# Conv + Fourier mixer + quantized FFN on one core: tokens parked in DRAM, two x buffers, and the forward sum over h in 64x64 tiles

## The chip, the cores and the metric

The kernel runs on one core of one Trainium2 chip. The metric is the device time of one launch in microseconds. All 32 images of the batch go through this one core.

## What is computed

The reference has two layers. Layer 0 is an inverted bottleneck with weights mixed per image; layer 1 is a Fourier mixer over the tokens and a feed-forward network (FFN) with numbers rounded to fp8 (e5m2). Cut to what matters:

```python
# x: (32, 56, 56, 96)
rw  = sigmoid(mean(x, (1, 2)) @ Wr + br)             # 4 routing weights per image
Wk  = einsum('be,ecm->bcm', rw, Wpw)                 # mixed pointwise weights
h   = relu(bn1(einsum('bhwc,bcm->bhwm', x, Wk)))     # 96 -> 384
h   = relu(bn2(depthwise3x3(h, mixed taps)))
x   = bn3(einsum('bhwm,bmf->bhwf', h, Wk2)) + x      # 384 -> 96, residual

t   = tokens(x)                                      # (32, 3136, 96)
a   = relu(bn(layernorm(t) @ w1.T))                  # 96 -> 192
X   = fft(a, axis=tokens, norm='ortho')
y   = ifft(relu(re) + 1j * relu(im), norm='ortho').real   # re, im: diagonal r, i, and biases
t   = t + bn(y @ w2.T)
t   = t + q_ffn(layernorm(t))                        # 96 -> 384 -> 96, fp8 operands
```

The Fourier transform over the 3136 = 56 x 56 tokens is done in two steps: a sum over h for each of the 56 columns w (29 frequencies, since the input is real), then a sum over w.

## The kernel before

**Layout.** x of an image lies as 96 channels x 3136 tokens in SBUF. There are three such buffers (`xpad`, `xs`, image b in buffer b % 3). Layer 0 overwrites x with its own output, the Fourier part adds to it, the FFN adds to it, and from there it is stored to the output. So a buffer belongs to one image from its load to the last store.

**Stages of one image**, each a Python generator that issues instructions:

- `loads` loads x; `mixing` sums x over the tokens on DVE (`pooled`), makes the routing weights (`ps_rw`), and the mixed weights `wk`, `small`, `wk2`.
- `expansion` (`ps_pw`), evicted by `expanded` into `hp`; the depthwise convolution partly on TensorE in 32x32 tiles (`convolved_tensor`, `ps_dw`) and partly on DVE (`convolved_vector`, `h2`); `projection` (`ps_pwl`), evicted by `projected`.
- `forward`, for four strips of 784 tokens: `moments` transposes the tokens (`ps_t_a`), takes `bn_stats` and makes one over the standard deviation (`rstd_a`). Then `ps_w1`: 112 tokens (two columns w) x 192. DVE scales and clips it into `ha`. Then `ps_a`: the sum over h with the matrix `dfta_s`. ACT copies it to `g`, and SP stores it to DRAM (`gd`).
- `frequency_loads` reads `gd` back in another order into `g2`; `frequencies` does the sum over w (`ps_b`), then `nonlinearity`, then `spectrum` (`ps_w2`, `ps_c`), stored to DRAM (`yd`).
- `inverse`: reads `yd` (`yt`), sums back (`ps_d`), adds it to x, normalizes (`ps_t_f`, `nt8`, `ps_n`), runs the FFN (`ps_f1`, `hidden`, `ps_f2`), adds it and stores the output.

**Order.** The order of the instructions on every engine is fixed when the program is built. `Plan.run` holds all generators, estimates when each could go on, and takes the one that can start first (priorities break ties). Inside one period, the convolution of image b stands among the forward part of b-1 and b, the frequency part of b-1 and the inverse of b-2. Every engine then works through its own queue in that order, held by semaphores.

**Padding.** PSUM has four tiles of two banks. `psum` takes one, and where `Plan` expects TensorE to be idle it first issues products that nobody reads:

```python
for _ in range(min(40, int((plan.idle() - 0.3) / 0.19))):
    nc.tensor.matmul(ps[:PB, 0:PB], dftb_s, dftb_s, start=True, stop=True)
```

**Lines.** Most instructions are issued by helpers, so the profile gives them one line: L553 is `mm`, L557 `transpose`, L321 the padding in `psum`, L282 every recorded instruction of DVE, ACT, POOL and SP. After the change the same helpers stand at L584, L588, L328 and L289.

**Before the loop**, the constants are loaded on the SP queue, among them the Fourier matrices `dfta_s` and `dftd_s` (1421 KB each). Scratch for this lies in the pool `prep`; the pools `mix` and `strip` are opened after `prep` is closed.

Of the kernel before, what the change touches and what calls it, by code (L numbers as in the profile page):

```python
# [56 lines left out]
PA = 4 * K1  # L57
KR = 2 * K1
# [3 lines left out]
SQ = SW // 2  # L62
T = SW * S
# [13 lines left out]
GK = 8  # L77
GROUPS = [(0, 16), (16, 13)]
# [52 lines left out]
class Plan:  # L131
# [8 lines left out]
    TAIL = {PE: 0.2, DVE: 0.12, ACT: 0.14, POOL: 0.1, SP: 0.0}  # L140

# [57 lines left out]
    def run(self):  # L199
        while self.streams:  # L200
            best = None
            for stream in self.streams:
                if any(len(self.buffers[tag]) < n for tag, n in stream.takes.items()):
                    continue
                ready = stream.ready
                missing = False
                for key in stream.after:
                    at = self.events.get(key)
                    if at is None:
                        missing = True  # L210
                        break
                    ready = max(ready, at)
                if missing:
                    continue
                for tag, n in stream.takes.items():
                    ready = max(ready, self.buffers[tag][n - 1])
                key = (max(ready, self.free[stream.engine]), stream.priority, ready)
                if best is None or key < best[0]:
                    best = key, ready, stream
            if best is None:  # L220
                raise RuntimeError(
                    "no stream can go on: "
                    + "; ".join(
                        f"{s.name} {[k for k in s.after if k not in self.events]} {s.takes}"
                        for s in self.streams
                    )
                )
            _, ready, stream = best
            has = self.free[PE]
            for tag, n in stream.takes.items():  # L230
                has = max(has, self.buffers[tag][n - 1])
                del self.buffers[tag][:n]
            self.gap = (has, ready) if stream.engine == PE else (0.0, 0.0)
            self.now = self.ready = ready
            self._advance(stream)
# [50 lines left out]
def kernel(  # L286
# [39 lines left out]
    xpad = [const([C, (S + 2) * S], F32, f"x_{i}") for i in range(min(3, NB))]  # L326
    xs = [xpad[b % 3][:, S : S + N] for b in range(NB)]
    for b in range(min(3, NB)):  # L328
        nc.gpsimd.memset(xpad[b][:, 0:S], 0.0)
        nc.gpsimd.memset(xpad[b][:, S + N :], 0.0)  # L330
# [3 lines left out]
    nc.sync.dma_start(xs[0], x[0])  # L334
    prep = tc.tile_pool(name="prep", bufs=1)
# [14 lines left out]
    dfta_s = const([PB, NQ, PA], F32, "dfta_s")  # L350
    nc.sync.dma_start(dfta_s, dfta)
    dftb_s = const([PB, PB], F32, "dftb_s")
    nc.sync.dma_start(dftb_s, dftb)
# [6 lines left out]
    for kind in range(NKIND):  # L360
        at = 128 * kind
        while at < 128 * kind + 128:

            ch, p = at % CH, at - 128 * kind
            h, c = divmod(ch, C)
            n = min(C - c, 128 - p)
            nc.sync.dma_start(w2_s[p : p + n, kind, at // CH, :], w2t[c : c + n, h, :])
            nc.sync.dma_start(nl_s[p : p + n, :, kind], in_vecs[c : c + n, :, h])
            at += n
    dftc_s = const([PB, PB], F32, "dftc_s")  # L370
    nc.sync.dma_start(dftc_s, dftc)
    dftd_s = const([PA, NQ, PB], F32, "dftd_s")
    nc.sync.dma_start(dftd_s, dftd)

# [6 lines left out]
    nc.vector.tensor_add(ident32, ident32, ident[:, 96:128])  # L381
    ident8 = const([PB, PB], E5M2, "ident8")
# [117 lines left out]
    f1 = pp.tile([C, M], F32, tag="f1", name="f1")  # L500
    nc.sync.dma_start(f1, fw1t)
    nc.vector.tensor_copy(fw1, f1, saturate=False)
    f2 = pp.tile([128, NC3, C], F32, tag="f2", name="f2")
    nc.sync.dma_start(f2, fw2t)
# [10 lines left out]
    mixp = ctx.enter_context(tc.tile_pool(name="mix", bufs=2))  # L515
# [23 lines left out]
    plan = Plan(ps=4, mir=2, zo=1, h16=4)  # L539
# [22 lines left out]
    mixed, small_of, wk2s, gds, yds, zs = {}, {}, {}, {}, {}, {}  # L562


    def loads():
        for b in range(NB):
            yield SP, [("out", b - 3, s) for s in range(NS) if b >= 3]
            if b:
                Q.dma_start(xs[b], x[b])
            arrives(4 * C * N if b else 0, "x", b)  # L570
# [71 lines left out]
    def expansion():  # L642

        for b, p, before in parts_of_all():
            xb = xpad[b % 3]
            for c in (2, 0, 1):

                for part, (at, ns) in enumerate((((0, (9, 9)), (18, (8, 8))), ((0, (8, 8)), (16, (9,))))[p]):
# [10 lines left out]
                    plan.spawn("evac pw", 5, expanded(b, p, c, part, at, ns, ps))  # L659
# [17 lines left out]
    def convolved_tensor():  # L677

        for b, p, before in parts_of_all():
            for i, wave in enumerate(WAVES[p]):  # L680
# [24 lines left out]
                plan.spawn("evac dw", 0, convolved(b, p, i, wave, ps))  # L705
# [41 lines left out]
    def projection():  # L747

        for b, p, _ in parts_of_all():
            needs = [("h2t", b, p, i) for i in range(len(WAVES[p]))] + [("wk2", b)]  # L750
            needs += [("h2v", b, p, c) for c, *_ in ON_VECTOR[p]]
            for s, blocks in (((0, (0, 1)), (1, (2, 3))), ((2, (4, 5)), (3, (6,))))[p]:
# [13 lines left out]
                plan.spawn("evac prj", 3, projected(b, s, blocks, ps))  # L766
            plan.done("prj", b, p)

    def projected(b, s, blocks, ps):
# [8 lines left out]
        plan.done("x1", b, s)  # L778

    def moments(name, xt, s, who, out, kept=None):  # L780
# [3 lines left out]
        for q in range(SQ):  # L784
            at = s * T + PB * q
            transpose(ps[:PB, 128 * q : 128 * q + C], xt[:, at : at + PB], ident[:C, :C])
        seen = slots(ps, PB, SQ, 128, C)
# [6 lines left out]

        st = sp.tile([PB, SQ, 6], F32, tag=f"st_{who}", name=f"st_{name}")
        for q in range(SQ):
            V.bn_stats(st[:, q, :], seen[:, q, :])
        if kept is None:
            plan.release()
        dm = sp.tile([PB, 2, SQ], F32, tag=f"dm_{who}", name=f"dm_{name}")  # L800
# [4 lines left out]
        W.behind.tensor_add(v, v, d)  # L805
        yield ACT
        rstd = sp.tile([PB, SQ], F32, tag=f"rstd_{who}", name=f"rstd_{name}")
        A.activation(rstd, v, AF.Sqrt, bias=eps_ln[:PB], scale=1.0 / C)
# [4 lines left out]
    def forward(parity):  # L813

        for b in range(NB):
            for s in range(parity, NS, 2):
                yield PE, [("x1", b, s)] + [("g2 read", b - 2)] * (b >= 2), 1
                if b not in gds:
                    gds[b] = dram.tile([PA, NQ, CH], F32, tag="gd", name=f"gd_{b}")
                xt, gd, got = xs[b], gds[b], []  # L820
                yield from moments(f"a_{b}_{s}", xt, s, f"a{parity}", got)
                rstd = got[1]
                for q0, nq in ((0, 4), (4, 3)):
                    yield PE, (), 1
                    ps = psum(f"ps_w1_{b}_{s}_{q0}")
                    for q in range(nq):
                        at = s * T + PB * (q0 + q)
                        mm(ps[:PB, 256 * q : 256 * q + CH], xt[:, at : at + PB], w1c)
                    yield DVE

                    ha = sp.tile([PB, 4, CH], F32, tag=f"ha{parity}", name=f"ha_{b}_{s}_{q0}")
                    for q in range(nq):
                        V.scalar_tensor_tensor(
                            ha[:, q, :],
                            ps[:PB, 256 * q : 256 * q + CH],
                            rstd[:, q0 + q : q0 + q + 1],
                            nshift[:PB],
# [6 lines left out]
                    for q in range(nq):  # L844
                        mm(ps[:PA, 256 * q : 256 * q + CH], dfta_s[:, s * SQ + q0 + q, :], ha[:, q, :])
                    yield ACT
                    g = sp.tile([PA, 4, CH], F32, tag=f"g{parity}", name=f"g_{b}_{s}_{q0}")
                    A.copy(g[:, 0:nq, :], slots(ps, PA, nq, 256, CH))
                    plan.release()
                    yield SP  # L850
                    at = s * SQ + q0
                    Q.dma_start(gd[0:PB, at : at + nq, :], g[0:PB, 0:nq, :])
                    Q.dma_start(gd[PB:PA, at : at + nq, :], g[PB:PA, 0:nq, :])
                arrives(4 * PA * 4 * CH, "g", b, s)

    def frequency_loads():
        n = 0
        for b in range(NB):
            for i, (k0, nk) in enumerate(GROUPS):
                yield SP, [("g", b, s) for s in range(NS)] + [("g2", n - 1)] * (n >= 1)  # L860
                Q.dma_start(
                    g2[:, 0:nk, :],
                    gds[b][4 * k0 : 4 * (k0 + nk)].rearrange("(k a) q m -> (a q) k m", a=4),
                )
# [4 lines left out]
    def frequencies():  # L869
# [4 lines left out]
        for b in range(NB):  # L874
            for i, (k0, nk) in enumerate(GROUPS):
                for kind in range(NKIND):
# [6 lines left out]
                    plan.spawn("nonlinearity", 3, nonlinearity(n, b, k0, size, kind, ps))  # L883
# [4 lines left out]
    def nonlinearity(n, b, k0, nk, kind, ps):  # L888
# [20 lines left out]
        plan.spawn("imaginary parts", 1, imaginary_parts(n, kind, im, zi, mi, rd, nr, used))  # L909
# [68 lines left out]
    def inverse(parity):  # L978


        for b in range(NB):
            for s in range(parity, NS, 2):
                yield SP, [("yd", b, i) for i in range(len(GROUPS))]
# [4 lines left out]
                arrives(4 * PA * SQ * C, "yt", b, s)  # L988
# [6 lines left out]
                strip = xs[b][:, s * T : s * T + T]  # L995
# [8 lines left out]
                yield from moments(f"f_{b}_{s}", xs[b], s, f"f{parity}", got, nt)  # L1004
# [24 lines left out]
                for c in range(NC3):  # L1029
# [8 lines left out]
                    plan.spawn("hidden", 0, hidden(parity, b, s, c, ps, h8))  # L1038
# [22 lines left out]
                arrives(4 * C * T, "out", b, s)  # L1061
# [15 lines left out]
    with tc.manual_schedule():  # L1077
        for name, priority, stream in (
            ("loads", 0, loads()), ("mixing", 5, mixing()), ("inverse", 3, inverse(0)),
            ("inverse", 0, inverse(1)), ("frequency loads", 4, frequency_loads()),  # L1080
            ("frequencies", 3, frequencies()), ("forward", 2, forward(0)),
            ("forward", 1, forward(1)), ("projection", 7, projection()),
            ("vector", 8, convolved_vector()), ("tensor", 6, convolved_tensor()),
            ("expansion", 9, expansion()),
        ):
            plan.spawn(name, priority, stream)
# [115 lines left out]
```

## Time and profile before

| What | Value |
|---|---|
| Median of 3 runs | 4445.54 us (4445.18 to 4452.17) |
| The profiled execution | 4452.19 us |
| Its span | 4450.0 us |
| PE / DVE / ACT / POOL busy | 4284.4 / 3512.3 / 2626.6 / 978.8 us |
| Granted TensorE clock | 0.994 |
| DMA, mean over the span | 76 GB/s |

A line of a group reads: source line, engine, operation, output <- inputs with shapes, count, then busy time and mean duration of one (ns), then the idle time of the engine before it and what ended that. Busy time of a group counts overlapping instructions once, so busy time over count is what one of them costs the engine, and the mean duration is longer than that where they overlap. A matrix product on f32 is two passes, and each is counted as one MATMUL. A line of a timeline reads: start, duration, engine, line, operation, and in brackets the idle time before it.

### The profile page before, as it was taken

What the parts mean: (1) busy time and instruction counts of PE and PEld (TensorE: products, weight loads), DVE (VectorE), ACT (ScalarE), POOL (GpSimd) and SP (SyncE); (2) the same over time, 40 slices, a digit from 0 to 9 for tenths busy, and PEclk for the clock granted to TensorE, in tenths of its full rate; (3) what the DMA queues carried; (4) which work ended last, traced back from release to release, by engine and by line L of the source; (5) the groups of instructions that cost most, each with busy time, mean ns of one, the idle gap of its engine ahead of it and who ended that gap; (6) DMA issues with size and microseconds to landing.
All of it is one profiled execution on the core that took longest, in us unless ns stands there. A gap on an engine that the chain in (4) does not pass through costs nothing.

```text
span 4450.0 us, 114927 instructions
## 1 busy us (share of the span) xinstructions
PE 4284.4 (96%) x48916; PEld 3152.2 (71%) x48916; DVE 3512.3 (79%) x7222; ACT 2626.6 (59%) x4135; POOL 978.8 (22%) x1012
## 2 busy tenths in 40 slices
PE   6999999999999999999999999999999999999998
PEld 4767677677777677777677777677777777776778
DVE  6768787788877888778888778888788888778863
ACT  2455666655656565656565666556566656566654
POOL 1011222122222122222222222212222212222222
PEclk9999999999999999999999999999999999999999
DMA  3222332222332322332322332322332322332221
GB/s 91 55 65 64 81 91 78 72 75 71 81 83 71 87 71 75 81 83 71 87 69 73 85 83 71 87 70 67 90 80 72 82 65 76 93 80 71 76 77 49
DMA packets 305448, 339.19 MB, mean 76 GB/s; under 512 B 127908, under 2 KB 244452, under 8 KB 301636
## 3 DMA queue, kind: packets, MB, share of 16 engines
q1 hardware_dynamic: 304936, 331.85, 28.2%
q8 instruction: 384, 6.29, 0.6%
q14 instruction: 128, 1.05, 0.1%
HBM read 164.06 MB, written 158.27 MB: 72 GB/s over the span
## 4 chain that ended last, share of the span: by engine, by line
PE 67%; DVE 13%; ACT 8%; DMA 7%; issue 4%; POOL 1%; SPq 1%; POOLq 0%; ACTq 0%; DVEq 0%
PE ps_dw L553 14%; PE ps_pwl L553 11%; PE ps_w L553 11%; PE ps_pw L553 8%; PE ps_a L553 5%; DVE h L282 5%; PE ps_b L553 4%; PE ps_f L553 4%; DMA x<-in_x_dram 4%; PE ps_c L553 2%; DMA yd<-zo 2%; ACT z L282 2%; DVE z L282 2%; ACT mir L282 2%; PE ps_t_f L557 2%
## 5 line engine op out<-in xcount | busy, mean ns | idle before, releaser
L282 DVE SCALAR_TENSOR_TENSOR h<-hp,small,h 128x1792 f32<-128x1792 f32 (+2 forms) x768 | 1292.9, 1683 | 47.6 <-ACT h L282 31.8
L553 PE MATMUL ps_dw<-hp,diag 32*32 32x448 f32 x27648 | 858.7, 543 | 14.7 <-issue 14.6
L553 PEld LDWEIGHTS ps_dw<-hp,diag 32*32 32x32 f32 x27648 | 537.2, 103 | 281.7 <-issue 96.6
L282 POOL CAST h<-h 128x784 fp8e5<-128x784 f16 x384 | 382.6, 1022 | 1181.6 <-DVE h L282 1181.6
L553 PE MATMUL ps_pw<-x,wk 96*128 96x448 f32 (+1 forms) x1344 | 571.2, 564 | 34.5 <-DVE z L282 33.9
L553 PE MATMUL ps_pwl<-h,wk 128*96 128x448 f32 x1344 | 526.3, 539 | 0.0
L282 ACT ACTIVATE hp<-ps_pw,small 128x896 f32<-128x896 f32 (+2 forms) x384 | 361.3, 953 | 268.0 <-PE ps_pw L553 267.7
L282 ACT ACTIVATE nt<-yt,nm,rstd_f 112x96 fp8e5<-112x96 f32 x896 | 334.5, 454 | 201.0 <-DVE nm L282 200.8
L553 PEld LDWEIGHTS ps_pw<-x,wk 96*128 96x128 f32 x1344 | 244.6, 190 | 259.5 <-issue 186.5
L282 POOL TENSOR_TENSOR x<-x,y 96x784 f32<-96x784 f32 x128 | 286.8, 2241 | 551.2 <-DVE y L282 528.2
L553 PEld LDWEIGHTS ps_w<-w_s,z 128*112 128x112 f32 (+1 forms) x2816 | 361.5, 181 | 56.0 <-issue 48.4
L553 PE MATMUL ps_w<-w_s,z 128*112 128x96 f32 (+2 forms) x2816 | 376.7, 288 | 9.8 <-issue 9.2
L282 ACT ACTIVATE h<-ps_dw,small 128x448 f32<-128x448 f32 x384 | 214.9, 630 | 288.0 <-PE ps_dw L553 288.0
L553 PEld LDWEIGHTS ps_pwl<-h,wk 128*96 128x96 f32 x1344 | 209.5, 163 | 239.5 <-issue 228.5
L282 DVE SCALAR_TENSOR_TENSOR ha<-ps_w,rstd_a,nshift 112x192 f32<-112x192 f32 x896 | 308.2, 408 | 86.6 <-PE ps_w L553 86.6
L553 PEld LDWEIGHTS ps_b<-dftb_s,g 112*128 112x128 f32 x2816 | 334.8, 192 | 15.9 <-issue 13.2
L553 PE MATMUL ps_w<-w1c,x 96*112 96x192 f32 x1792 | 329.6, 329 | 9.9 <-ACT h L282 7.1
L553 PE MATMUL ps_b<-dftb_s,g 112*128 112x112 f32 x2816 | 339.0, 274 | 0.0
L553 PE MATMUL ps_a<-ha,dfta_s 112*116 112x192 f32 x1792 | 329.6, 330 | 7.7 <-ACT hp L282 7.4
L553 PEld LDWEIGHTS ps_a<-ha,dfta_s 112*116 112x116 f32 x1792 | 286.0, 181 | 36.5 <-ACT hp L282 31.0
L553 PEld LDWEIGHTS ps_w<-w1c,x 96*112 96x112 f32 x1792 | 284.6, 177 | 37.2 <-ACT h L282 18.9
L282 ACT ACTIVATE z<-ps_b,nl_s 128x448 f32<-128x448 f32 (+2 forms) x384 | 248.7, 689 | 88.3 <-PE ps_b L553 88.0
(160 smaller groups left out, 6197.7 us busy)
## 6 DMA issues: line engine op xcount, KB each, us to landing
gd<-g SPq DMA_DIRECT2D x128, 336.0 KB
g<-gd SPq DMA_DIRECT2D x32, 1344.0 KB
x<-in_x_dram SPq DMA_DIRECT2D x32, 1176.0 KB
yt<-yd SPq DMA_DIRECT2D x128, 294.0 KB
out_dram<-x SPq DMA_DIRECT2D x128, 294.0 KB
g<-gd SPq DMA_DIRECT2D x32, 1092.0 KB
gd<-g SPq DMA_DIRECT2D x128, 252.0 KB
yd<-zo SPq DMA_DIRECT2D x96, 336.0 KB
```

The source lines that it names most:

```text
L282: return getattr(self.namespace, name)(out, *args, **kw)
L553: nc.tensor.matmul(to, lhsT, rhs, start=start, stop=stop)
L557: nc.tensor.transpose(to, ap, eye)
```

## The change

The change has several parts.

1. **Two buffers of x.** `xpad` has two instead of three. `projected` stores the tokens after layer 0 to DRAM (`x1s`); `inverse` reads them strip by strip into one of four strips (`x1`, `NX1 = 4`), and adds and stores from there. `loads` waits for the last read of x by `ps_w1` and for the stores to DRAM of image b-2, instead of for the outputs of image b-3.
2. **The sum over h in four tiles of 64x64.** Each of the two columns w of a group of 112 tokens gets its own 64 partitions (8 + 56). `ps_w1` becomes two products of 64 columns each, into partitions 0 to 63 and 64 to 127. `ps_a` becomes, for two groups, four products of 64 rows x 64 (or 58) columns. `dfta_s` is repacked once on POOL. `moments` takes a strip by start and length; the variance is brought into the new partitions with one small product with the constant `spread`. The strips of `forward` are now 8, 8, 8 and 4 groups long (`FWD`). `gd` has a new layout, and two DMAs instead of one read each group of `g2`.
3. **Constants.** `dfta`, `dftc` and `dftd` are loaded last; `dftb_s`, `w2_s` and `nl_s` on the ACT queue; `f1` and `f2` before the Fourier matrices. The pool `mix` is opened before `prep`.
4. **Order.** New priorities of the generators and of what they spawn, and `SLACK`, by which `Plan` assumes that an engine starts a little after it comes free.

```diff
+    SLACK = {PE: 0.05, DVE: 0.2, ACT: 0.1, POOL: 1.2, SP: 0.0}
...
-                key = (max(ready, self.free[stream.engine]), stream.priority, ready)
+                at = max(ready, self.free[stream.engine] + self.SLACK[stream.engine])
+                key = (at, stream.priority, ready)
...
-    xpad = [const([C, (S + 2) * S], F32, f"x_{i}") for i in range(min(3, NB))]
-    xs = [xpad[b % 3][:, S : S + N] for b in range(NB)]
+    xpad = [const([C, (S + 2) * S], F32, f"x_{i}") for i in range(2)]
+    xs = [xpad[b % 2][:, S : S + N] for b in range(NB)]
...
+    mixp = ctx.enter_context(tc.tile_pool(name="mix", bufs=2))
     prep = tc.tile_pool(name="prep", bufs=1)
...
-    dfta_s = const([PB, NQ, PA], F32, "dfta_s")
-    nc.sync.dma_start(dfta_s, dfta)
...
-    nc.sync.dma_start(dftb_s, dftb)
+    for c in range(2):
+        for i in range(2):
+            for odd in range(2):
+                to, at = NQ * (2 * c + i) + odd, NQ * (2 * (c ^ odd) + i) + odd
+                nc.scalar.dma_start(dftb_s[to : to + NQ - odd : 2, :], dftb[at : at + NQ - odd : 2, :])
+    f1 = pp.tile([C, M], F32, tag="f1", name="f1")
+    nc.sync.dma_start(f1, fw1t)
+    f2 = pp.tile([128, NC3, C], F32, tag="f2", name="f2")
+    nc.sync.dma_start(f2, fw2t)
...
+    spread = const([PB, 2 * SP64], F32, "spread")
+    nc.gpsimd.memset(spread, 0.0)
+    for r in range(2):
+        at = SP64 * r + 8
+        nc.vector.tensor_copy(spread[:, at : at + S], ident[:PB, S * r : S * r + S])
...
+    dfta_all = pp.tile([128, NQ, PA], F32, tag="dfta_all", name="dfta_all")
+    nc.gpsimd.memset(dfta_all, 0.0)
+    for r in range(2):
+        nc.sync.dma_start(dfta_all[SP64 * r + 8 : SP64 * r + SP64], dfta[S * r : S * r + S])
+    dfta_s = const([128, NQ, SP64], F32, "dfta_s")
...
+        nc.gpsimd.tensor_copy(
+            dfta_s[at, :, 0:KR].rearrange("p q (k i) -> p q k i", i=2),
+            dfta_all[at].rearrange("p q (k r i) -> p q k r i", r=2, i=2)[:, :, :, r, :],
+        )
...
-            yield SP, [("out", b - 3, s) for s in range(NS) if b >= 3]
+            yield SP, [(key, b - 2, s) for s in range(NS) for key in ("x read", "x1 by") if b >= 2]
...
+        yield SP
+        if b not in x1s:
+            x1s[b] = dram.tile([C, N], F32, tag="x1", name=f"x1_{b}", bufs=3)
+        at = slice(blocks[0] * TB, (blocks[-1] + 1) * TB)
+        Q.dma_start(x1s[b][:, at], xs[b][:, at])
...
+        if kept is None:
+            yield PE
+            np_ = 2 * SP64
+            mm(ps[:, C : C + n], spread, v)
+            v = ps[:, C : C + n]
...
-                    for q in range(nq):
-                        at = s * T + PB * (q0 + q)
-                        mm(ps[:PB, 256 * q : 256 * q + CH], xt[:, at : at + PB], w1c)
+                    for q in range(4):
+                        for r in range(2):
+                            at = S + PB * (lo + q0 + q) + S * r - 8
+                            mm(
+                                ps[SP64 * r : SP64 * r + SP64, 256 * q : 256 * q + CH],
+                                xpad[b % 2][:, at : at + SP64],
+                                w1c,
+                                share=2,
+                            )
...
-                    for q in range(nq):
-                        mm(ps[:PA, 256 * q : 256 * q + CH], dfta_s[:, s * SQ + q0 + q, :], ha[:, q, :])
+                    for q in range(0, 4, 2):
+                        for odd in range(2):
+                            for r in range(2):
+                                c = r ^ odd
+                                at = slice(SP64 * r, SP64 * r + SP64)
+                                to = 512 * odd + 128 * q
+                                m = KR if c else SP64
+                                mm(
+                                    ps[SP64 * c : SP64 * c + m, to : to + CH],
+                                    dfta_s[at, lo + q0 + q + odd, 0:m],
+                                    ha[at, q + odd, :],
+                                    share=3.3,
+                                )
...
-                Q.dma_start(
-                    g2[:, 0:nk, :],
-                    gds[b][4 * k0 : 4 * (k0 + nk)].rearrange("(k a) q m -> (a q) k m", a=4),
-                )
+                for c in range(2):
+                    Q.dma_start(
+                        g2[S * c : S * c + S, 0:nk, :],
+                        gds[b][c, 2 * k0 : 2 * (k0 + nk)].rearrange("(k i) q m -> (i q) k m", i=2),
+                    )
...
+                strip = sp.tile([C, T], F32, tag="x1", name=f"x1_{b}_{s}", bufs=NX1)
+                Q.dma_start(strip, x1s[b][:, s * T : s * T + T])
...
-                strip = xs[b][:, s * T : s * T + T]
...
-            ("loads", 0, loads()), ("mixing", 5, mixing()), ("inverse", 3, inverse(0)),
-            ("inverse", 0, inverse(1)), ("frequency loads", 4, frequency_loads()),
-            ("frequencies", 3, frequencies()), ("forward", 2, forward(0)),
-            ("forward", 1, forward(1)), ("projection", 7, projection()),
-            ("vector", 8, convolved_vector()), ("tensor", 6, convolved_tensor()),
-            ("expansion", 9, expansion()),
+            ("loads", 8, loads()), ("mixing", 6, mixing()), ("inverse", 1, inverse(0)),
+            ("inverse", 0, inverse(1)), ("frequency loads", 0, frequency_loads()),
+            ("frequencies", 1, frequencies()), ("forward", 0, forward(0)),
+            ("forward", 0, forward(1)), ("projection", 7, projection()),
+            ("vector", 5, convolved_vector()), ("tensor", 2, convolved_tensor()),
+            ("expansion", 7, expansion()),
```

The arguments `share` are only estimates for `Plan`; they change no instruction.

## The prediction, as put on record before the changed kernel was run

> **What bounds the kernel now.** I read the page's first lines first.
>
> ```profile
> span 4450.0 us, 114927 instructions
> PE 4284.4 (96%) x48916; PEld 3152.2 (71%) x48916; DVE 3512.3 (79%) x7222; ACT 2626.6 (59%) x4135; POOL 978.8 (22%) x1012
> ```
>
> TensorE (PE) is busy 96% of the span, so only what shortens PE's queue or its waits counts. But part of that busy time is padding: the `dftb_s` x `dftb_s` products of `psum` (L321), whose results nobody reads. The second view is busy time by windows, first of everything, then of L321 alone; columns are window, its length, then PE, PEld and so on.
>
> ```profile
> 823.00:956.00 133.00, 129.92 (x1501) 95.01 (x1500) 109.10 (x224) 81.92 (x129) 30.50 (x31) 1.00 0.30 78
> ...
> 823.00:956.00 133.00, 6.68 (x58) 6.10 (x58) 1.00 0.30 78
> ```
>
> One image takes 133 us. Of PE's 129.9 us, 6.7 are padding (29 products of two passes), and 3.1 us are idle. DVE has 109.1 us: not the bound, but near enough to cause waits. The timeline around an image's end says what the padding covers.
>
> ```profile
> 1177.19 0.49 SPq L282 DMA_DIRECT2D x<-in_x_dram  x1
> ...
> 1185.29 3.42 DVE L282 TENSOR_REDUCE pooled<-x 96x1 f32<-96x3136 f32 x1 [0.26 <-DMA x<-in_x_dram]
> ...
> 1186.04 1.36 PE L321 MATMUL ps_c<-dftb_s 112*112 112x112 f32 x12
> ...
> 1189.17 0.36 PE L553 MATMUL ps_rw<-wr_s,pool_b 96*128 96x4 f32 x2 [0.41 <-DVE pool_b L282]
> 1189.38 1.80 PE L321 MATMUL ps_w<-dftb_s 112*112 112x112 f32 x16
> ...
> 1193.17 1.16 PE L321 MATMUL ps_c<-dftb_s 112*112 112x112 f32 x10
> ...
> 1195.51 1.75 PE L321 MATMUL ps_pw<-dftb_s 112*112 112x112 f32 x16
> 1197.10 6.57 PE L553 MATMUL ps_pw<-x,wk 96*128 96x504 f32 x16
> ```
>
> The next x is loaded only at 1177, because `loads` waits for the outputs of b-3; then come 8.1 us of DMA, `pooled`, `ps_rw`, the mixing of `wk`, and at last the expansion (`ps_pw`). All padding of the image lies on this chain. In the whole program L321 has 1383 products, in 315.9 us busy (sum of its groups): 0.228 us each.
>
> The costs to price the new matrix work come from the groups (the profile drops numbers in names: `ps_w<-w1c` is `ps_w1`).
>
> ```profile
> L553 PE MATMUL ps_dw<-hp,diag 32*32 32x448 f32 x27648 | 858.7, 543 | 14.7 <-issue 14.6
> L553 PE MATMUL ps_pwl<-h,wk 128*96 128x448 f32 x1344 | 526.3, 539 | 0.0
> L553 PE MATMUL ps_a<-ha,dfta_s 112*116 112x192 f32 x1792 | 329.6, 330 | 7.7 <-ACT hp L282 7.4
> L553 PE MATMUL ps_w<-w1c,x 96*112 96x192 f32 x1792 | 329.6, 329 | 9.9 <-ACT h L282 7.1
> L553 PE MATMUL ps_rw<-wr_s,pool_b 96*128 96x4 f32 x64 | 10.9, 241 | 26.1 <-issue 17.1 <-DVE pool_b L282 8.8
> ```
>
> Every f32 product is two passes. A pass of 448 columns over the full array takes 526.3/1344 = 0.392 us of PE; sixteen 32x32 tiles together take 16 x 858.7/27648 = 0.497. Tiles do run side by side, at 1.27 times a lone pass.
>
> **What the Trainium skill says.** "TensorE: Matmul & The Clock Gate", section Measured speedup vs the span model: 3 column tiles gain 2.38x, 16 tiles 10.6x. Here sixteen give 16/1.27 = 12.6x; two or four the trace does not show. "TensorEngine Tiling (Array Packing)", Key Properties: a change of tiling mode drains the array. It agrees: the first `ps_dw` pass at 956.42 starts about 0.09 us later than the last `ps_w1` pass (956.165, passes 0.162 apart) would allow. "DMA: Bandwidth & Descriptors", Issuing engines are not separate DMA queues: all share 16 engines. In 1124-1128 one g2 load alone shows a DMA share of 1.1, so two large loads at once do collide.
>
> **The change, part by part**, per image where not said. The order of both programs' instructions can be counted without running them.
>
> *Padding.* 466 L321 products remain of 1383; from the third image to the last but one there is none. -917 x 0.228 = **-209 us** (whole run). This is no assumption on waits: they are instructions. What may come back is wait time, priced below.
>
> *Sums over h (`ps_a`).* 28 full products become 14 groups of four 64x64 tiles, so 28 waves of passes instead of 56 passes of 329.6/1792 = 0.184 us (10.3 us). A wave costs 1.0 to 1.27 passes; I take 1.12: 5.8 us, **-4.5** (-5.2 to -3.8).
>
> *Projection to 192 (`ps_w1`).* 28 products of 112 columns become 56 of 64 columns in two column tiles: the same number of waves, factor 1.0 to 1.27, taken 1.05: **+0.5** (0 to +2.8).
>
> *Mode changes.* The order has 14 such groups, and 22 boundaries between modes more than before: 22 x 0.093 = **+2.0** (1 to 3).
>
> *The `spread` product in `moments`.* Four more, two passes each at the 10.9/64 = 0.17 of `ps_rw`: **+1.4** (1 to 2). It waits for DVE's variance, and PE's whole queue stands behind it; between `ps_t_a` and it lie other products (`ps_pwl`, `ps_d`, or `ps_f1`), of 1 to 5 us, against 8 `bn_stats` of 0.25 and four ops of 0.17, 2.7 us. Its PSUM buffer, one of four, is held until the square root. DVE's `ha` grows in partitions only, the ACT copies of g fall from 8 to 7: nothing.
>
> *Priorities and `SLACK`* issue nothing; they only choose the order, which is what I read the gaps from.
>
> *x in two buffers, tokens through DRAM.* 8 more DMAs for x1 (4 stores, 4 loads), 2 x 1176 KB, so about 12.8 MB per image instead of 10.4 (78 GB/s x 133 us): share 0.30 to about 0.37, not a bound on average. SP issues 8 DMAs more for x1 and 2 for g2, 2 fewer for gd at 0.3 to 0.5 us each, while it mostly waits: hidden. The x1 reads go out with yt, after yd lands, and need 294 KB more beside yt's 304: the inverse comes up to 2 us later, under about 10 us of `ps_pw`, `ps_pwl` and `ps_t_a` that stand before `ps_d`. The x load now waits for the last `ps_w1` and the x1 stores of b-2, in mid-image, and `ps_rw` is 20 us behind (12 needed: 8.1 load, 3.7 DVE). Behind the waiting load on SP stand the last gd writes; behind `pooled` on DVE, which comes after 11 us of `h16` and `h2`, stand `y16` and the nonlinearity: both waits fit by 3 us. So the chain of the third view is gone; its waits at `ps_rw` and `ps_c`, 3.6 us in the five images from 823 to 1495, go with it: **-0.7**.
>
> *What is late next.* The x load now goes out just before the last gd writes and the g2 load that needs them. In the new order `ps_f1` x12 (2.3), `ps_a` (0.9), `ps_dw` (8.9), `ps_f2` x12 (2.3), `ps_pw` x2 (1.7) stand between the last `ps_w1` and `ps_b`: 16.1 us. Needed, if the gd write queues behind x: 8.1 + 1.5 to land + 8.6 for g2 (as from 1121.8 to 1130.4) = 18.2. **+2.1** (0, if they interleave well, to +5).
>
> *Start.* The first mixing is held by this:
>
> ```profile
> 47.25 0.36 SPq L504 DMA_DIRECT2D f<-in_fw2t_dram  x1
> ...
> 50.04 0.10 POOL L282 MEMSET rw<- 128x1 f32 x1 [39.89 <-DVE fw L505]
> ...
> 53.84 0.56 PE L553 MATMUL ps_rw<-wr_s,pool_b 96*128 96x4 f32 x2 [17.13 <-issue]
> ```
>
> `rw` takes room that `prep` frees, and the last user of `prep` waits for f2, queued behind 18 us of `dftd_s`. After, `mix` is opened first and f1, f2 go ahead of the Fourier matrices; then PE can do `ps_rw` when its padding ends (36.7): **-17 us once**. At worst -8: SP's six `stk_s` turns now stand behind `dfta`, `dftc`, `dftd` in its queue, POOL's `diag` behind two copies that wait for `dfta` (10.4 us to land). ACT's 20 new DMA issues lie in its idle time up to 11.7. The tail (image 31) keeps 388 of 406 padding products: counted above, otherwise unchanged.
>
> **Sum.** Per image -4.5 + 0.5 + 2.0 + 1.4 - 0.7 + 2.1 = +0.8, x 32 = +26. Total -209 + 26 - 17 = -200. The profiled execution took 4452.2 us (span 4450.0), 6.7 above the median of 4445.5: 4252 on its scale, **4246** as a median.
>
> **Rivals.**
> 1. *Better overlap* (0.2): tiles cost 1.0, half the drains, no wait for g2: -0.7 - 0.5 - 1.0 - 2.1 = -4.3 per image, -138: 4108. For it: 16 tiles lose 27%, so four may lose little.
> 2. *A wait in place of the padding* (0.2): x, gd and g2 collide fully (+2.9), and DVE, then 109 of 131 us, delays `ps_pw` and `spread` by some 1.2 more: +4.1, +131: 4377. For it: the order leaves PE no reserve. Against: the longest waits now total 3.1 us.
> 3. *The column tiles of `ps_w1` do not overlap* (0.06), slower: every pair then costs two passes, +10.3 instead of +0.5, +314: 4560. It decides from +6.2 per image, when over 60% of the second tile's passes stand alone. Against: in `ps_dw`, column tiles of one row group do run together.
> 4. *The tokens' way through DRAM delays `ps_d`* by over 6 us at each image's start (0.04): 4450 or more. Against: DMA share 0.30.
>
> That the padding goes cannot fail; that its time comes back as waits is rival 2.
>
> **How the numbers follow.** The likeliest case has 0.5, range 4180 to 4310. 8 in 10 need most of rivals 1 and 2: 4110 to 4385. A measurement here tells about 0.2% (9 us) from no change: faster 0.90, same 0.02, slower 0.08 (rivals 3 and 4, less a little).
>
> **What would show it.** `ps_a` about 185 us busy, `ps_w1` near 345; L321 near 106; PE idle about 4.5 us per image, most before `ps_b`; an image at about 127 us; first `ps_pw` at about 44 us. I am wrong if `ps_w1` shows over 500 us, if `ps_d` or `ps_rw` waits for a DMA, or if an image still takes 131 us.

## The result, and the profile after

The changed kernel takes **4959.2 us** (median of 4 runs, 4951.7 to 4960.6) against 4447.7 us before (4 runs beside it): ratio 1.1145, 95% interval 1.1126 to 1.1165. It is 511 us slower where 200 us less were forecast; the range (4110 to 4385) does not hold it. The page of its profiled execution (4960.2 us) begins:

```profile
span 4958.4 us, 119614 instructions
PE 4308.4 (87%) x50922; PEld 2926.4 (59%) x50922; DVE 3459.4 (70%) x7224; ACT 2600.3 (52%) x4103; POOL 1092.5 (22%) x1015
```

PE is busy 87% instead of 96%: its idle time went from 166 to 650 us. So the forecast's matrix work is not the first suspect. The groups of PE say the same (the last line is `ps_b` of the kernel before; `ps_dw` of before, 858.7 us, stands in the prediction):

```profile
L584 PE MATMUL ps_dw<-hp,diag 32*32 32x448 f32 x27648 | 948.8, 581 | 116.4 <-ACT g L289 107.2 <-issue 3.7 <-DVE rw L289 3.1
L584 PE MATMUL ps_b<-dftb_s,g 112*128 112x112 f32 x2816 | 427.0, 322 | 295.7 <-DMA g<-gd 293.0 <-ACT zo L289 2.2 <-DVE z L289 0.4
...
L584 PE MATMUL ps_w<-w1c,x 96*64 96x192 f32 x3584 | 340.0, 332 | 2.4 <-ACT g L289 1.4 <-ACT rstd_a L289 0.8
L584 PE MATMUL ps_a<-ha,dfta_s 64*58 64x192 f32 (+1 forms) x3584 | 196.8, 334 | 0.4 <-ACT h L289 0.2
...
L553 PE MATMUL ps_b<-dftb_s,g 112*128 112x112 f32 x2816 | 339.0, 274 | 0.0
```

The two new kinds of product cost about what was forecast (`ps_w1` 340 us for 345, `ps_a` 197 for 185). But `ps_dw` and `ps_b`, the same products as before, are 90 and 88 us longer, and they wait. From the list of waits, these bear on it:

```profile
PE ps_b L584 <- DMA g<-gd: 293.0, 32, 12.7
ACT g L289 <- DMA gd<-g: 264.0, 84, 10.7
PE ps_dw L584 <- ACT g L289: 107.2, 41, 4.2
PE ps_w L584 <- ACT h L289: 71.7, 28, 2.9
DVE pooled L289 <- DMA x<-in_x_dram: 63.5, 30, 7.7
```

The columns are us in all, times, and the longest; the fourth line is `ps_w2`. The first three belong together. A copy to `g` waits until the write of the tile before it (`gd<-g`) has landed. Meanwhile PSUM stays taken, and `ps_dw` stands. In the end the load of `g2` (`g<-gd`) comes late at `ps_b`, once an image. The chain of waits through one such place (start, us, what):

```profile
2108.99 0.81 ACT g L289
...
2110.09 9.55 DMA gd<-g
...
2119.73 0.81 ACT g L289
...
2120.82 15.43 DMA gd<-g
...
2136.27 7.35 DMA g<-gd
...
2143.76 6.29 PE ps_b L584 x28
```

A write of two times 58 rows that the prediction took for 1.5 us is 9.6 and 15.4 us under way. The DMA view of a stretch in which such writes are nearly all that moves (2046 to 2054 us) shows why. The last number of the line `q1` is the DMA share, the mean busy share of the core's 16 DMA engines:

```profile
DMA packets 143, 0.43 MB, mean 54 GB/s; under 512 B 6, under 2 KB 6, under 8 KB 142
...
q1 hardware_dynamic: 142, 0.42, 12.9%
...
gd<-g SPq DMA_DIRECT2D x4, 174.0 KB
```

12.9% of 16 engines is two engines. The start and length of each packet in this trace say the same: two packets are under way for 7.6 of the 8 us, three for the rest, never more. At 54 GB/s a tile's 348 KB (two DMAs) take 6.6 us, and several tiles in a row queue up. The Trainium skill, "DMA: Bandwidth & Descriptors", section Why a DMA increments its semaphore by 16 and not by 1, states the rule: a DMA runs on the largest number of engines up to 16 that divides the outermost dimension of both its sides. Here that is the number of rows. 58 = 2 x 29 leaves two engines, as the trace shows; 112, the large part of a tile before, is divisible by 16.

Last, the clock. The first line below begins near the end of a wait of 3.4 us before `ps_dw`; the second holds the end of the wait of 8.2 us before `ps_b` and what follows it. The last three numbers of a window are the granted clock, the DMA share and GB/s:

```profile
2119.50:2126.30 6.80, 5.71 (x115) 2.93 (x129) 5.22 (x5) 2.23 (x3) 4.74 (x4) 0.50 0.28 98
2140.00:2150.20 10.20, 6.44 (x30) 6.47 (x31) 0.90 (x3) 1.86 (x3) 0.68 (x1) 0.50 0.74 206
```

After both waits TensorE works at half its clock for a while. In the whole span the clock records show 0.5 for 630 us in 89 stretches (before: 57 us in 12). Of `ps_b`'s 427 us 187 fall into them, of `ps_dw`'s 949 us 137, and of `ps_w2`'s 412 us 85.

### The profile page after: what moved, and what is told of

Its sections match the earlier page's. It is cut to its first block, busy times and chain, and to the rows that moved or that the text cites. A ratio compares the mean times of both kernels' runs of the same rounds, so it can differ in the third digit from the quotient of the medians.

```text
span 4958.4 us, 119614 instructions
## 1 busy us (share of the span) xinstructions
PE 4308.4 (87%) x50922; PEld 2926.4 (59%) x50922; DVE 3459.4 (70%) x7224; ACT 2600.3 (52%) x4103; POOL 1092.5 (22%) x1015
## 4 chain that ended last, share of the span: by engine, by line
PE 43%; DMA 29%; DVE 11%; ACT 11%; issue 3%; POOL 2%; SPq 1%; ACTq 0%; POOLq 0%; DVEq 0%
DMA gd<-g 23%; PE ps_pwl L584 7%; PE ps_w L584 7%; PE ps_pw L584 7%; PE ps_dw L584 6%; PE ps_b L584 5%; DMA g<-gd 5%; DVE h L289 4%; PE ps_d L584 3%; ACT nt L289 3%; ACT h L289 3%; DVE z L289 2%; POOL h L289 2%; ACT g L289 2%; PE ps_c L584 1%
## 5 line engine op out<-in xcount | busy, mean ns | idle before, releaser
L584 PE MATMUL ps_dw<-hp,diag 32*32 32x448 f32 x27648 | 948.8, 581 | 116.4 <-ACT g L289 107.2
L289 POOL CAST h<-h 128x784 fp8e5<-128x784 f16 x384 | 542.2, 1433 | 1433.5 <-DVE h L289 1433.5
L584 PE MATMUL ps_b<-dftb_s,g 112*128 112x112 f32 x2816 | 427.0, 322 | 295.7 <-DMA g<-gd 293.0
L584 PEld LDWEIGHTS ps_b<-dftb_s,g 112*128 112x128 f32 x2816 | 410.9, 235 | 333.7 <-issue 330.2
L584 PE MATMUL ps_w<-w_s,z 128*112 128x96 f32 (+2 forms) x2816 | 411.9, 306 | 72.5 <-ACT h L289 71.7
L289 POOL TENSOR_TENSOR mir<-mir,z 128x448 f32<-128x448 f32 (+1 forms) x192 | 204.1, 1063 | 855.5 <-ACT mir L289 758.5
L584 PE MATMUL ps_w<-w1c,x 96*64 96x192 f32 x3584 | 340.0, 332 | 2.4 <-ACT g L289 1.4
L289 ACT COPY g<-ps_a 122x768 f32<-122x768 f32 x224 | 179.1, 800 | 301.8 <-DMA gd<-g 264.0
L289 ACT CAST h<-ps_f 128x784 f16<-128x784 f32 x384 | 292.7, 820 | 84.6 <-PE ps_f L584 82.1
L289 DVE SCALAR_TENSOR_TENSOR ha<-ps_w,rstd_a,nshift 128x192 f32<-128x192 f32 x896 | 309.7, 408 | 24.8 <-PE ps_w L584 20.7
```

Source lines behind the costliest of these rows:

```text
L289: return getattr(self.namespace, name)(out, *args, **kw)
L584: nc.tensor.matmul(to, lhsT, rhs, start=start, stop=stop)
```

## The experiments

**Theory A**: the 58-row writes run on two engines; their waits, and the half clock behind them, are the loss. **Theory B**: the x load, the gd writes and the g2 load meet at one place, and their volume is the loss. Where no number of runs is given, the kernel ran once, and its time has no interval; it is set beside the median of before on the same chip (4451.0, 4454.6, 4448.6 and 4447.7 us in the four groups of runs).

**1. 64 rows.**

```diff
-                    gds[b] = dram.tile([2, KR, NQ, CH], F32, ...
+                    gds[b] = dram.tile([2, SP64, NQ, CH], F32, ...
...
-                                m = KR if c else SP64
+                                m = SP64
...
-                        Q.dma_start(gd[c, :, at : at + 4, :], g[SP64 * c : SP64 * c + KR])
+                        Q.dma_start(gd[c, :, at : at + 4, :], g[SP64 * c : SP64 * c + SP64])
```

> Both halves of gd get 64 rows instead of 58 (the ps_a products write 64 rows each, the copy to g takes 128, each of the two DMAs of a g tile 64); every order stays. Theory A (a DMA of 58 rows keeps only 2 of the 16 engines busy: 116 packets take 7 us alone and 10 to 15 us in a group, and the g2 load and the copies to g wait for them): the DMA share in the windows of the gd writes rises from 0.13 to over 0.5, the wait of ps_b for the g2 load falls from 293 us to under 100, that of the ACT copies g for gd<-g from 264 to under 40, the granted clock is back above 0.98, the time 4200 to 4330. Theory B (the volume: x load, gd writes and g2 load meet at one place): 10% more bytes at the same place, so 4900 to 5000 as after.

Measured: 4414.5 us (4 runs), ratio to before 0.9927 (0.991 to 0.9943); clock 0.990; `ps_b` waits 32.0 us for `g2`; ACT no longer waits for `gd<-g` at all. It moves more bytes and takes 545 us less than the changed kernel. Theory B falls. But the time is 85 us above the upper end of what A expected, so something else in the forecast is wrong too.

**2. No x load.** `if b:` ahead of the load becomes `if b == 1:`, so that from the third image on no x is loaded.

> After, with the x loads left out from the third image on (the images compute on what the buffers hold: that part of the computation is left out); gd keeps its 58 rows. Theory A: the gd writes still run at a DMA share of about 0.13 and take 7 us and more; only the 8 us in which the x load stands ahead of the last of them go: about 4700 to 4900. Theory B (meeting the x load is the cost): ps_b waits under 100 us in all, 4200 to 4350.

Measured: 4869.2 us. The writes of gd still have a DMA share of 0.13, and `ps_b` still waits 245.2 us. The meeting with x, which the prediction had priced as the only collision, is some 90 us of the loss.

**3. The kernel before with 58 rows.**

```diff
-                    Q.dma_start(gd[0:PB, at : at + nq, :], g[0:PB, 0:nq, :])
-                    Q.dma_start(gd[PB:PA, at : at + nq, :], g[PB:PA, 0:nq, :])
+                    Q.dma_start(gd[0:KR, at : at + nq, :], g[0:KR, 0:nq, :])
+                    Q.dma_start(gd[KR:PA, at : at + nq, :], g[KR:PA, 0:nq, :])
```

> The kernel before with one thing changed: the 116 rows of a g tile are written as 58 and 58 instead of 112 and 4 (same bytes, same number of DMAs). Theory A: the copies to g and the g2 loads begin to wait in this kernel too: 4600 to 4950, PE waits before ps_b of over 150 us. Theory B: nothing changes by over 0.5%, 4425 to 4470.

Measured: 5448.4 us, 22% more than before, with nothing but the split of the rows changed (`PB` is 112, `PA` 116, `KR` 58). That is A's direction, at twice the upper end of its size. The waits of PE in it:

```profile
PE ps_d L553 <- DMA yt<-yd: 302.4, 31, 10.2
PE ps_b L553 <- DMA g<-gd: 238.5, 31, 8.4
PE ps_dw L553 <- ACT g L282: 99.5, 29, 4.3
```

The second and third are those of after. The first is new: here the reads of `yd` come late as well. That they stand behind the writes on the same two engines fits, but no run tests it apart.

**4. The kernel before with 60 and 56 rows.** As 3, split at row 60.

> The kernel before with its g tiles written as 60 and 56 rows instead of 112 and 4 (with 58 and 58 it took 5448): same bytes, same number of DMAs, same order. If rows are dealt to the largest divisor of their number up to 16 (15 and 14 engines): 4435 to 4470. If to powers of two (4 and 8): 4700 to 5100. If writing in two nearly equal halves was itself the loss: 5300 to 5500.

Measured: 4453.7 us, as before. So the two halves as such are not the cause. By the rule 60 and 56 rows go to 15 and 14 engines; in the packet records mostly 8 to 15 of these packets are under way at once, where in run 3 it is mostly two.

**5. 60 rows in the changed kernel.** As 1, with `KR + 2` for the rows.

> As after, with 60 rows in each half of gd instead of 58 (two more rows of zeros are computed, copied and written); every order stays. If the rows go to as many engines as the largest power of two that divides their number (2 for 58, 4 for 60, 16 for 64): DMA share about 0.25 in the writes, a lone tile 3 to 4 us, 4440 to 4650. If they go to the largest divisor up to 16 (2 for 58, 15 for 60): as with 64 rows, 4395 to 4430. If it is neither and 60 rows go as 58: 4900 to 5000.

Measured: 4398.3 us, 0.9874 of the median of before beside it. In a stretch of writes (2017 to 2019.5) its DMA view reads:

```profile
DMA packets 150, 0.39 MB, mean 155 GB/s; under 512 B 28, under 2 KB 28, under 8 KB 149
...
q1 hardware_dynamic: 149, 0.37, 45.5%
```

45.5% on average over bursts is more than the 4 of 16 engines (25%) that a power of two would give, and in the bursts mostly 10 to 15 packets are under way. Two rows more in each half of gd, which nobody needs, take 561 us off the changed kernel. Its page and groups, to be set beside those of the changed kernel:

```profile
PE 4128.4 (94%) x50922; PEld 2776.2 (63%) x50922; DVE 3482.6 (79%) x7224; ACT 2597.8 (59%) x4103; POOL 1098.6 (25%) x1015
...
L584 PE MATMUL ps_dw<-hp,diag 32*32 32x448 f32 x27648 | 882.0, 545 | 31.1 <-issue 24.0 <-DVE rw L289 4.9 <-ACT g L289 0.3
...
L584 PE MATMUL ps_b<-dftb_s,g 112*128 112x112 f32 x2816 | 360.5, 289 | 31.7 <-DMA g<-gd 23.5 <-ACT h L289 6.5 <-ACT hp L289 1.4
```

**6. Two g buffers**, with 58 rows: `bufs=2` for the tag of `g`.

> After with 58 rows, and two buffers for each of the two g tags, so that a copy to g seldom waits for the write of the one before. Theory A in two channels (the copies to g hold PSUM and with it ps_dw, 107 us; the g2 load comes late at ps_b, 293 us): the waits of ACT g and of ps_dw for g go to under 20 us, the wait at ps_b stays over 200 us, since the writes themselves are as slow: 4780 to 4920. Rival (the waiting copies are what makes the writes late): ps_b under 120 us, 4400 to 4550.

Measured: 4853.3 us, 106 less than with one buffer. No wait of ACT for `gd<-g` is left in the list, and none of `ps_dw` for `g`, but `ps_b` waits 392.5 us instead of 293.0. This is what A expects: buffers move a part of the wait, they don't speed the writes.

**7. One DMA of 128 rows.** Once as it stands, and once with the planner told of an issue that isn't there (the last line, in the second kernel only), so that the order on PE is that of run 1, product for product.

```diff
-                    for c in range(2):
-                        Q.dma_start(gd[c, :, at : at + 4, :], g[SP64 * c : SP64 * c + SP64])
+                    Q.dma_start(gd[:, :, at : at + 4, :].rearrange("c r q m -> (c r) q m"), g)
+                    plan.tick(SP, 0.36)
```

> As the kernel with 64 rows in each half, but a g tile is written by one DMA of 128 rows instead of two of 64: 28 DMA issues of SP in an image become 14 of gd. If the number of issues on SP (some 0.4 us each) delays the x load or the g2 load, 10 to 60 us less than with two DMAs; if SP has time, within 10 us of it. Theory B: 4900 to 5000.

> One DMA of 128 rows for each g tile, as in the kernel that took 4696, but the planner is told of the issue that is gone, so that the order on every engine stays that of the kernel with two DMAs of 64 rows (4414.5). Theory A: the transfers are as good (a lone tile of 128 rows took 1.2 us at a DMA share of 1.0), and the 280 us of the kernel with one DMA came from another order of work: 4380 to 4430 here. Rival: one DMA of 128 rows is the slow part: 4650 to 4740.

Measured: 4696.1 us (4 runs, ratio 1.0563, 1.0543 to 1.0583) and 4418.1 us. The transfers are the same in both. The 278 us between them come from the order that `Plan` makes when SP comes free 0.36 us earlier: images of 132 to 155 us in turn, with 215 padding products more. The first of the two expectations did not see this coming. So undoing one part of this change does not weigh that part, unless the order is held.

**8. Old priorities**, on the kernel with 60 rows, `SLACK` all zero.

> The kernel with 60 rows (4398), with the priorities of the kernel before and SLACK at zero: the same instructions, another order. If the order is what most of the gain over before now hangs on: 4550 to 4850, with the loss as waits of PE. Rival (the order matters little beside the instructions saved): 4380 to 4440.

Measured: 4713.1 us. The same work on the images in another order takes 315 us more, so the gain of the 60-row kernel over before hangs on the new order. The loss is not waits of PE alone, as was expected: PE is idle for 338 us instead of 268, its padding grows by 582 products (238 us instead of 103), and the clock is at 0.5 for 370 us instead of 88.

**9. The kernel before without padding.**

```diff
-            for _ in range(min(40, int((plan.idle() - 0.3) / 0.19))):
+            for _ in range(0 * int(plan.idle())):
```

> The kernel before without its 1383 padding products; everything else, the order too, as before. The prediction's step (padding costs its own busy time, 0.228 us each): 316 us of products go; even if only the 209 us of those in steady state are gained, 4240, with PE's idle time as before (166 us). Rival (most padding stands where PE waits for ACT or DVE anyway, and the wait is seen once the padding is gone): idle time rises by 150 to 300 us, the granted clock falls below 0.99, 4400 to 4470.

Measured: 4476.6 us (4 runs), ratio **1.0065 (1.0048 to 1.0082)**: 1383 products less make it a little slower. The page and the list of waits:

```profile
PE 4140.7 (93%) x46150; PEld 2948.6 (66%) x46150; DVE 3511.9 (79%) x7222; ACT 2628.2 (59%) x4135; POOL 979.8 (22%) x1012
```

```profile
PE ps_c L553 <- ACT zo L282: 100.6, 66, 2.9
PE ps_pw L553 <- DVE z L282: 33.8, 30, 1.4
...
PE ps_w L553 <- issue: 22.6, 9, 3.0
PE ps_d L553 <- DMA yt<-yd: 15.2, 7, 6.7
```

PE's busy time falls by 144 us only, not by 316, and its idle time rises by 165. The clock is 0.963, with 331 us at 0.5 instead of 57. `ps_c` now waits 100.6 us for ACT (13.3 before), where padding stood. And the same `ps_pw` products take 623 us instead of 571.

**10. Padding in the longest wait of the changed kernel** (58 rows).

```diff
                     ps = psum(f"ps_b_{b}_{k0}_{kind}")
+                    for _ in range(36 if i == 0 and kind == 0 else 0):
+                        nc.tensor.matmul(ps[:PB, 0:PB], dftb_s, dftb_s, start=True, stop=True)
```

> After (58 rows), with 36 padding products (8.2 us) put ahead of the first ps_b product of each image, where PE waits 8 to 9 us for the g2 load: 1152 products of work more. If PE's idle time is what brings the clock down (0.5 in the stretches after the wait, ps_b 14.4 us an image instead of 10.6, the projection after it 13.2 instead of 11.6), the clock rises from 0.936 to 0.96 or more, ps_b falls to 11 to 12 us, and the time by 3 to 5 us an image: 4800 to 4870. Rival (the clock falls for another reason, so padding only takes time where it is longer than the wait): 4950 to 5000.

Measured: 4905.6 us (4 runs; ratio to before 1.1039, 1.1013 to 1.1065, against 1.1145 without). 1152 products more make it some 54 us faster; the clock is 0.965. Its groups:

```profile
L584 PE MATMUL ps_b<-dftb_s,g 112*128 112x112 f32 x2816 | 361.7, 290 | 63.0 <-DMA g<-gd 60.1 <-ACT zo L289 2.3 <-DVE z L289 0.4
...
L954 PE MATMUL ps_b<-dftb_s 112*112 112x112 f32 x2304 | 231.8, 262 | 0.0
```

`ps_b` is 65 us shorter, as expected, and between the two profiled executions (spans of 4958.4 and 4892.7 us) that is the whole gain. PE's idle time and this padding together are 651 us, as long as the idle time without it (650), so the padding took no time of its own. The time gained is 1.7 us an image instead of the 3 to 5 expected. The waits before `ps_dw` (111 us) and `ps_w2` (73 us), with half clock behind them, are still there (346 us at 0.5), and `ps_w2`, which was expected to gain too, takes 409 us for 412. In direction the first expectation holds: a TensorE that stands idle loses its clock, and work that nobody reads keeps it.

The Trainium skill, "TensorE: Matmul & The Clock Gate", Part 1: The HAM clock gate, says that the clock is at half after an idle window of some 3.4 us. The length agrees with that: 81 of the 89 stretches at 0.5 in the changed kernel are 3.4, 6.8 or 10.2 us long. But the measurement goes beyond the page: such a window need not be idle throughout. In the 3.4 us ahead of these 89 stretches TensorE was busy for 0 to 2.4 us, 0.8 in the median, and ahead of the 53 of run 9 for 0 to 2.2 us, 1.6 in the median. So shorter waits cost the clock as well; those of `ps_c` in run 9 are 2.9 us at most.

**11. The start.** Two tries: `row_s` ahead of `x[0]` (on the kernel with 64 rows), and the loads of `w2_s` and `nl_s` back on SP's queue (on that with 60).

> The kernel with 64 rows, and row_s loaded ahead of x[0] instead of behind it. The first ps_rw of after stood at 46.6 us instead of about 37, because ps_w1c waits until 35.6 for a chain that starts with row_s, issued at 9.1 us: if that is so, ps_w1c starts 6 to 9 us earlier, the first ps_rw at 37 to 41, and the time is 5 to 9 us under 4414.5 (4405 to 4410). Rival: x, then 5 us later, delays pooled instead, and nothing is gained (4410 to 4420).

> The kernel with 60 rows, and the 12 loads of w2_s and nl_s on SP's queue as before, instead of ACT's; the order on PE, DVE and POOL stays (save a few first instructions). If the start was held by ACT (its first Sqrt stood behind its own DMA issues until 16.6 us, DVE waited for nl_s until 21.7): ps_w1c starts at 27 to 31 us instead of 36, the first ps_rw at 37 to 41, and the time is 5 to 9 us under 4398. Rival (12 issues more on SP delay wpwl_s, f1, dfta by as much): 4394 to 4402.

Measured: the first takes 4432.4 us (5 runs, ratio 0.9951, 0.9932 to 0.997), with the first `ps_rw` at 44.2 us for 45.8 in run 1: no gain in time is seen. The second takes 4403.6 us (4 runs; ratio **0.9893, 0.9876 to 0.991**), with the first `ps_rw` at 38.1 us. What had held it, in the timeline of ACT after the change:

```profile
16.08 0.45 ACTq L383 DMA_DIRECT2D nl_s<-in_vecs_dram  x1
16.56 1.28 ACT L434 ACT_TABLE_LOAD   x1 [16.56 <-issue]
17.86 0.52 ACT L434 ACTIVATE s1row<-s1row 96x384 f32<-96x384 f32 x1
22.23 0.39 ACT L434 ACTIVATE s<-s 128x3 f32<-128x3 f32 x3 [3.85 <-DVE s L433]
```

ACT's Sqrt stood behind its own 20 DMA issues, and DVE waited 6.1 us for the `nl_s` that they bring. With 12 of them on SP the mixing starts 9 us earlier than in the 60-row kernel (47.3 us); whether the end moves by as much can't be told from these runs, as the 60-row kernel has only one. This version is faster than both the kernel before (by 1.1%) and the changed kernel.

## Why the prediction was wrong, step by step

- **"1.5 to land" for a gd write: the failing step, some 560 us.** The writes were priced by the number of issues ("hidden") and by bytes over all 16 engines ("not a bound on average"), not by the rows of each DMA. Measured were 9.6 and 15.4 us where 1.5 stood. Runs 1, 3, 4 and 5 show it. With 60 rows, idle time is 268 us instead of 650, and `ps_dw`, `ps_b` and `ps_w2` are 174 us shorter. The second part is the clock: at 0.5 these three groups have 409 us in the changed kernel and 57 with 60 rows, and half of the difference is 176 us. So both halves of the loss, waits and clock, go with the slow writes. The sign could have been read from before: the load of `dftd_s` has 116 = 4 x 29 rows and ran on four engines (37 to 41 us, DMA view of before; its packet records show four packets under way nearly throughout):

```profile
DMA packets 32, 0.40 MB, mean 100 GB/s; under 512 B 0, under 2 KB 0, under 8 KB 0
...
q1 hardware_dynamic: 32, 0.40, 25.9%
```

- **Padding, -209, "no assumption on waits": wrong.** The products went as counted (L328 has 104 us for 106). But that this is time saved is an assumption on waits: the products cost their time only if PE would otherwise work. In the kernel before, taking all of them out costs 0.65%. How much of the 209 us the changed kernel saves, no run shows. Rival 2's title, a wait in place of the padding, names what run 9 shows, though it gave other waits.
- **Priorities and `SLACK` "issue nothing": true of the work on the images, but they are worth more than any step of the sum.** Run 8 puts 315 us on them, and run 7 puts 278 us on a shift of 0.36 us. They also set how much padding `Plan` puts in: with the old ones 1048 products of it stand in the 60-row kernel, with the new ones 466. So over half of the padding that goes, goes by the order.
- **`ps_a`, `ps_w1`, `spread`, mode changes: right, or near.** 197 us for 185, 340 for 345, 40 for 45. Rival 3 falls. By the shapes of the products, the 60-row kernel changes the tiling mode (the tiles into which the array is cut) 30 times an image and the kernel before 8 times: the 22 more that were counted. In the kernel before, the product after the last pass of a `ps_w1` starts 0.16 us later where the mode stays and 0.26 us later where it changes. In the 60-row kernel it always changes there, and the step is 0.26 us. That is near the 0.093 of the forecast.
- **Collision at `ps_b`, +2.1 per image:** with 60 rows the wait is 23.5 us in all, 0.7 per image. It was in the step's range (0 to 5).
- **Tokens through DRAM:** `ps_d` waits 12.1 us for `yt` in the whole of the changed kernel. Rival 4 falls.
- **Start, -17:** it gained 9 us (first `ps_pw` at 52.2 us instead of 61.2). The step "ACT's 20 new DMA issues lie in its idle time up to 11.7" failed: they lasted until 16.5. In the last version of run 11 the first `ps_pw` stands at 43.6 us, for 44 forecast.
- **What is left:** the 60-row kernel is 146 us above the forecast span of 4250. About half is idle time: +102 us against before (166 to 268), where the forecast had +28 (the waits -0.7 and +2.1 times 32, the start -17; mode changes counted as busy). Most of them are waits of up to 1.5 us for ACT, POOL and DVE at `ps_w2`, `ps_f2`, `ps_t_f` and `ps_f1`. The rest is busy time: `ps_dw`, `ps_pw`, `ps_f1` and `ps_b` are 21 to 29 us longer each than before. `ps_b` has 49 us at half clock, which is enough for its 21 us; `ps_dw` and `ps_pw` come in more and shorter pieces (152 and 313, where before has 107 and 196). No run takes this apart, and how the gain of 56 us is shared between the new products and the new order stays open.

## What to carry to other kernels

Price a DMA by the number of its outermost rows before its bytes: a layout of 58 rows left an eighth of the engines here, and two rows that nobody needs were a cheap fix. Padding that fills a wait is no cost to be saved, as run 9 shows; price the wait first. Where a planner orders the work, hold its order when you test one part, or you measure another order.

## What the hardware showed that was not expected

- Rows and engines: 58 rows ran at a DMA share of 0.129 and 54 GB/s, 116 rows at 0.259 and 100 GB/s. The packets of a lone tile of 128 rows (393 KB) in run 7 took 1.1 us, with a share of 1.0 in the middle of it.
- An idle TensorE pays twice: in the image from 2000 us, the wait of 8.2 us at `ps_b` was followed by `ps_b` products of 14.4 us, where an image before has 10.6.
- Half the clock came after 3.4 us windows in which TensorE had worked for up to 2.4 us, so a wait need not fill such a window.
- POOL's cast of `h` takes 1444 ns in the 60-row kernel and 1022 before, with the same shape. No run asks why.
